# Depthwise sums of the last six jobs in PSUM banks, with two of their taps multiplied and added by GpSimd

## The chip, the core and the metric

The kernel runs on one core of one Trainium2 chip. The metric is the device time of one execution in microseconds. Engines are named as in the profile: PE (TensorE), DVE (VectorE), ACT (ScalarE), POOL (GpSimd), SP (SyncE); PEld is PE's weight load, and SPq is SP's queue of transfers.

## The reference

The input is 16 images of 128 channels and 96x96 pixels, in float32. Each image goes through one block: a normalisation over the channels, an attention over channels, a second normalisation, and a feed-forward part with a 3x3 depthwise convolution. Both halves add their result to their input.

```python
x_hwc = x.transpose(0, 2, 3, 1)
xn1 = _layernorm(x_hwc, ln1_w, ln1_b)
attn_out = _attention(xn1, wq, wk, wv, wp)       # 8 heads, softmax over a 16x16 matrix per head
x = x + attn_out.transpose(0, 3, 1, 2)
xn2 = _layernorm(x.transpose(0, 2, 3, 1), ln2_w, ln2_b).transpose(0, 3, 1, 2)
# _ffn: 128 -> 512 channels, 3x3 depthwise on 512, exact gelu, 512 -> 128 channels
h1 = jnp.einsum('bchw,oc->bohw', xn2, w_in[:, :, 0, 0])
h2 = lax.conv_general_dilated(h1, w_dw, (1, 1), ((1, 1), (1, 1)), feature_group_count=512, ...)
h3 = jax.nn.gelu(h2, approximate=False)
x = x + jnp.einsum('bchw,oc->bohw', h3, w_out[:, :, 0, 0])
```

## The kernel before

Channels lie on the 128 partitions. An image is cut into 8 bands of 12 rows (1152 pixels), a band into 3 units of 4 rows (384 pixels); the 16 images give 128 bands. The 512 hidden channels are 4 chunks of 128. A *job* is one chunk of one band, that is one depthwise convolution of 128x1152 values; there are 450 jobs, since in 62 of the 128 bands the fourth chunk is done by PE instead (L968, nine matmuls per unit with the first layer's weights folded into the taps). The last two bands are of that kind, so the last six jobs are chunks 0 to 2 of these two bands.

*Normalisations.* Both norms, called a (first) and b (second), run over groups of 512 pixels. PE transposes four blocks of 128 pixels into a PSUM tile `pT` (L610); DVE takes the statistics of two blocks at a time (`st`, L617); POOL adds the epsilon (L624) and raises to the power -1/2 (`rstd`, L628); for norm b DVE makes the shift (`nb`, L632). ACT writes the scaled blocks to SBUF (`zT`, L664 for a, L668 for b), and PE transposes three blocks back into a PSUM tile `pB` (`back`, L715), from which ACT places them in the padded input `xn` of the next stage (L721 for a, L719 and L725 for b). In norm a, PE also adds up the matrix of channel products (L678).

*PSUM.* There are eight banks of 512 float32 per partition. Two are the turning buffers of the pool `p_tr` (the tiles `pT`), one is the pool `p_bk` (`pB`), four are the tiles `h_0` to `h_3` that matmuls share, and one holds the products of norm a:

```python
p_tr = ctx.enter_context(tc.tile_pool(name="p_tr", bufs=2, space=PSUM))
p_bk = ctx.enter_context(tc.tile_pool(name="p_bk", bufs=1, space=PSUM))
...
d["pT", q] = p_tr.tile([P, QT, P], F32, tag="tr", name=f"pT_{name}_{q}")
...
d["pB"] = p_bk.tile([P, UT], F32, tag="bk", name=f"pB_{name}_{u}")
```

*A job.* PE multiplies the input with the chunk's weights (`hidden`, L900), ACT evicts the result to a padded tile (`kept`, L905). The nine taps of the convolution are shifted views of that tile; the first layer's weights are scaled so that tap 0 has the factor 1. DVE adds the taps one after the other with a multiply-and-add (`tap`, L918), the first of them onto tap 0. Taps 1 and 2 are multiplied by ACT (`product`, L913) into SBUF tiles `pr` and added by accumulating DMAs that POOL issues (`add_products`, L922: tap 2's product onto tap 1's, then the sum onto DVE's sum). DVE does six taps in each job, and eight in the very last, which has no DMA taps. Then ACT takes the gelu in place (L926), PE multiplies the four chunks with the output weights (`ffn_out`, L991), and the result is added to the residual, by ACT's copy (L1003) and a DMA (L1006), or in the last two bands by DVE (`add_here`, L998). SP stores the band.

*Order.* Nothing is left to a run-time scheduler. `Plan` collects every operation with its engine, a planned duration, a place in the order (the table `AT`), its reads and its writes, plays them through in planned time, and hands out buffer slots. The operations are then emitted in the order of their planned starts, and each engine works through its own list in that order. The waits between engines are put in by the framework when the program is built: it follows which instruction touches which tile, and adds a semaphore wait where two engines' uses of a tile must not overlap.

Of the kernel before, what the change touches and what calls it, by code (L numbers as in the profile page):

```python
# [18 lines left out]
BR = 12  # L19
PE_CHUNK = 3  # L20
PE_BANDS = (0, 2, 4, 6, 8, 10, 12)
PE_OF = 15
PE_LAST = (0, 1, 2, 4, 5, 7)
TINY = 1e-20
UNIT_MIN = 1e-18
DMA_TAPS = (1, 2, 3)
THIRD, THIRD_OF, THIRD_CHUNK = (), 3, 1
PART, Z_PARTS = 24, 6
QT, QB = 4, 1
# [11 lines left out]
    add_x_0=-281.3, gram_0=-43.8, forth_a_0=-74.3, forth_b_0=1.05, stats_a_0=-30.2, stats_b_0=-254.35,  # L41
    scaled_a_0=-88.5, scaled_b_0=171.2, back_a_0=-144.35, back_b_0=-18.9, place_a_0=-142.05, place_b_0=49.7,
    shift_b_0=-116.3, late=-68.9,
)
STEP = dict(scaled=0.3, hidden=0.1, products=0.5, tap=0.166, conv=1.6, conv_tap=0.03, out=0.8, out_part=0.05)
SLACK = 300
# [4 lines left out]
T_VARIANCE = 420  # L51
T_POWER = 1000
T_ADD, T_MOVE = 3100, 1800


class Plan:
# [154 lines left out]
def tile_restormer_block(  # L211
# [24 lines left out]
    nc = tc.nc  # L236
    B, C, H, W = x.shape
    P = 128
# [3 lines left out]
    UT = UR * W  # L242
# [11 lines left out]
    const = ctx.enter_context(tc.tile_pool(name="const", bufs=1))  # L254
    xpool = ctx.enter_context(tc.tile_pool(name="xpool", bufs=XB_BUFS))
    x1pool = ctx.enter_context(tc.tile_pool(name="x1pool", bufs=X1_BUFS))
    p_tr = ctx.enter_context(tc.tile_pool(name="p_tr", bufs=2, space=PSUM))
    p_bk = ctx.enter_context(tc.tile_pool(name="p_bk", bufs=1, space=PSUM))
    p_h = ctx.enter_context(tc.tile_pool(name="p_h", bufs=1, space=PSUM))
    p_g = ctx.enter_context(tc.tile_pool(name="p_g", bufs=1, space=PSUM))  # L260

    xbs, x1s = {}, {}
    banks = [p_h.tile([P, 4 * P], F32, name=f"h_{k}") for k in range(H_BANKS)]


# [20 lines left out]
    ratio = const.tile([P, NCH, 9], F32, name="ratio")  # L286
# [22 lines left out]
    prp = ctx.enter_context(tc.tile_pool(name="prp", bufs=PR_BUFS))  # L309
# [39 lines left out]
    op = plan.op  # L349

    def at(kind, place, i=1):
        return place + AT[kind if i else kind + "_0"]
# [25 lines left out]
    def dve(ns, p, f, r, w, two=False):  # L378
        op("DVE", ns, p, f, r, w, ns + 120 + SLACK, ns + 120, two=two)
# [7 lines left out]
    def act(ns, p, f, r, w):  # L387
        op("ACT", ns, p, f, r, w, ns + 150 + SLACK, ns + 150)
# [162 lines left out]
    def norm(i, second, place_of):  # L551
# [41 lines left out]
        def pixels(s, m):  # L593
# [8 lines left out]
            def forth(q):  # L602
                if early:
                    d["pT", q] = bank((name, q)).rearrange("p (t c) -> p t c", c=P)
                else:
                    d["pT", q] = p_tr.tile([P, QT, P], F32, tag="tr", name=f"pT_{name}_{q}")
                for k in range(QT):
                    b, j = divmod(q * QT + k, TPB)
                    xt = (xbs if x_key(i, b, second) == "xb" else x1s)[i, b]
                    nc.tensor.transpose(d["pT", q][:, k, :], xt[:, j * P : (j + 1) * P], ident)  # L610
# [96 lines left out]
        def channels(s, u):  # L707

            d = {}

            def back():
                d["pB"] = p_bk.tile([P, UT], F32, tag="bk", name=f"pB_{name}_{u}")
                for j in range(TPU):
                    q, k = divmod(u * TPU + j, QT)
                    nc.tensor.transpose(d["pB"][:, j * P : (j + 1) * P], zTs[q][:, k, :P], ident)  # L715

            def place():
                if second:
                    nc.scalar.activation(interior(i, u), rows(d["pB"]), AF.Identity, bias=b2)  # L719
                else:  # L720
                    nc.scalar.copy(interior(i, u), rows(d["pB"]))  # L721

            def place_row(k, r, row):
                to = window(xns[k], r, 1, 1)
                nc.scalar.activation(to, rows(d["pB"])[:, row : row + 1, :], AF.Identity, bias=b2)  # L725

            copies = []
            if second and u % UPP == 0 and u > 0:
                copies.append((part_of(i, u * UR - 1)[0], PART + 1, 0, UPP))
            if second and u % UPP == UPP - 1 and u < NU - 1:  # L730
                copies.append((part_of(i, (u + 1) * UR)[0], 0, UR - 1, -1))

            pb = ("bk", (name, u))
            quads = {(u * TPU + j) // QT: None for j in range(TPU)}
            pe(110 * TPU, at("back" + ab, s, i), back, [(*zt_of(q), k) for q in quads for k in range(2)], [pb])
            act(t_act(UT, 1) - 43 if second else t_copy(UT), at("place" + ab, s, i), place, [pb, ("w", "shift")], [z_unit(i, u)])
            for k, r, row, of in copies:
                act(225, at("place" + ab, s, i), lambda k=k, r=r, row=row: place_row(k, r, row), [pb, ("w", "shift")], [("z", k, of)])
# [138 lines left out]
    def h3_of(g, n):  # L877
        if (g, n) not in h3s:
            h3s[g, n] = h3p.tile([P, BR, W], F32, tag="h3", name=f"h3_{g}_{n}")
        return h3s[g, n]  # L880

    def conv_job(j, g, n):

        i, b = divmod(g, NB)
        kz, r0 = part_of(i, b * BR)
        xn = xns[kz]
        d = {}
        jn = (g, n)
# [14 lines left out]

        def kept(r, e):
            nc.scalar.copy(window(h1_, r, e - r, 1), rows(d.pop(("ph", r))))  # L905

        def shifted(t):
            dy, dx = divmod(t, 3)
            return window(h1_, dy, BR, dx)

        def product(t):
            to = d["pr", t] = prp.tile([P, BR, W], F32, tag="pr", name=f"pr_{g}_{n}_{t}")
            nc.scalar.activation(to, shifted(t), AF.Copy, scale=ratio[:, n, t : t + 1])  # L913

        def tap(t):
            h3 = h3_of(g, n)
            onto = shifted(0) if t == left[0] else h3
            nc.vector.scalar_tensor_tensor(h3, shifted(t), ratio[:, n, t : t + 1], onto, ALU.mult, ALU.add)  # L918

        def add_products(t):  # L920
            to = d["pr", DMA_TAPS[0]] if t != DMA_TAPS[0] else h3_of(g, n)
            nc.gpsimd.dma_start(out=to, in_=d["pr", t], accum_op=ALU.add)  # L922

        def gelu(s0, s1):
            h3 = h3_of(g, n)[:, s0 * UR : s1 * UR, :]
            nc.scalar.activation(h3, h3, AF.Gelu)  # L926

        last = j == len(jobs) - 1
        third = n == THIRD_CHUNK and g % THIRD_OF in THIRD
        dma_taps = () if last else DMA_TAPS[: 3 if third else 2]  # L930
        left = [t for t in range(1, 9) if t not in dma_taps]
        h1 = [("h1", n, k) for k in range(4)]
        h3 = [("h3", jn, s) for s in range(UPB)]
        for k, (r, e) in enumerate(chunks):
            ph = ("h", (jn, r))
            jk, zs = j + STEP["hidden"] * k, z_units(kz, r0 + r, r0 + e)
            to = h1[k + 1 : k + 2] if r else h1[:2]
            pe(t_mm((e - r) * W), at("hidden", jk), lambda r=r, e=e: hidden(r, e), [*zs, ("w", "in")], [ph])
            act(t_copy((e - r) * W), at("kept", jk), lambda r=r, e=e: kept(r, e), [ph], to)
        for k, t in enumerate(dma_taps):  # L940
            jk = j + STEP["products"] * k
            act(t_act(BR * W, 1), at("products", jk), lambda t=t: product(t), h1, [("pr", (jn, t))])
        pr = [("pr", (jn, t)) for t in dma_taps]
        for k, t in enumerate(dma_taps[1:]):
            add(at("add_last", j), lambda t=t: add_products(t), [pr[1 + k]], [pr[0]])
        for k, t in enumerate(left):
# [143 lines left out]
```

## Time and profile before

| what | value |
|---|---|
| runs | 4182.61 and 4180.88 us, median 4181.74 |
| the profiled execution, its span | 4197.8 us |
| mean granted clock of PE | 0.996 |
| busy: PE | 4120.2 us, 98% |
| busy: DVE | 4089.8 us, 97% |
| busy: ACT | 3697.8 us, 88% |
| busy: POOL | 2606.6 us, 62% |
| DMA | 831.16 MB, mean 198 GB/s |

The span is counted from the first to the last instruction of one profiled execution; it is 16 us longer than the median of the runs. Busy shares are of the span. A row of the groups reads: line, engine, operation, what is written and read with the shapes, count, then total busy time and the mean duration of one in ns, then the idle time of the engine just before these instructions and what ended it. A row of the timeline reads: start and length in us, engine, line, operation, tiles, count; equal instructions that follow each other are one row.

### The profile page before, as it was taken

The numbers are of one execution on the slowest core, as the hardware profiler recorded it, in microseconds if no ns is written. First come the engines' busy times: TensorE is split into PE (matmuls) and PEld (weight loads), VectorE is DVE, ScalarE is ACT, GpSimd is POOL, SyncE is SP. The second block draws the span as 40 slices with busy tenths as digits, with TensorE's granted clock in tenths as the row PEclk, the third lists the DMA queues.
The fourth block names the chain that finished last, engine by engine and source line by source line (L and its number), as shares of the span: only waits on it lengthen the run. The fifth ranks groups of instructions, "written<-read, shape, count | busy, mean of one in ns | idle before, by whom it ended". The sixth has DMA issues, their size and how long they took to land.

```text
span 4197.8 us, 52159 instructions
## 1 busy us (share of the span) xinstructions
PE 4120.2 (98%) x17265; PEld 2648.1 (63%) x17265; DVE 4089.8 (97%) x4450; ACT 3697.8 (88%) x7232; POOL 2606.6 (62%) x2397
## 2 busy tenths in 40 slices
PE   8999999999999999999999999999999999999999
PEld 6666666666666666656666666666666666665555
DVE  6999999999999999999999999999999999999998
ACT  5899988999899888889899989998899888999885
POOL 4757666565666757767576565666656666675442
PEclk9999999999999999999999999999999999999999
DMA  3899999999999999999999999999999999999997
GB/s 91 178 195 213 194 215 196 198 203 204 205 206 202 209 193 205 198 211 202 195 210 205 204 203 199 210 199 210 200 204 208 194 212 200 201 203 191 196 190 167
DMA packets 204797, 831.16 MB, mean 198 GB/s; under 512 B 23664, under 2 KB 25072, under 8 KB 204528
## 3 DMA queue, kind: packets, MB, share of 16 engines
q0 software_dynamic: 165024, 676.01, 83.3%
q1 hardware_dynamic: 37152, 151.01, 9.8%
q8 instruction: 137, 2.24, 0.2%
q10 hardware_dynamic: 2352, 0.81, 0.1%
q14 instruction: 132, 1.08, 0.1%
HBM read 148.26 MB, written 75.50 MB: 53 GB/s over the span
## 4 chain that ended last, share of the span: by engine, by line
PE 59%; DVE 27%; ACT 5%; POOL 4%; DMA 2%; issue 2%; ACTq 0%; POOLq 0%; DVEq 0%
DVE h L918 24%; PE h L968 16%; PE h L991 15%; PE h L900 12%; PE g L678 4%; PE h L567 4%; PE pB_a L715 2%; PE pT_b L610 2%; PE pB_b L715 2%; PE pT_a L610 2%; DVE st_a L617 1%; DMA h<-pr 1%; DVE st_b L617 1%; ACT pr L913 1%; POOL rstd_b L628 1%
## 5 line engine op out<-in xcount | busy, mean ns | idle before, releaser
L918 DVE SCALAR_TENSOR_TENSOR h<-h,ratio,h 128x1152 f32<-128x1152 f32 x2252 | 3105.2, 1403 | 4.1
L913 ACT ACTIVATE pr<-h,ratio 128x1152 f32<-128x1152 f32 x898 | 1159.8, 1296 | 44.0 <-DMA h<-pr 29.8
L968 PE MATMUL h<-xn,comp 128*128 128x384 f32 x3348 | 1195.2, 486 | 2.5 <-ACT h L905 2.5
L991 PE MATMUL h<-h,woutT 128*128 128x384 f32 x3072 | 1138.7, 488 | 5.8 <-ACT h L926 2.8
L900 PE MATMUL h<-xn,winT 128*128 128x384 f32 (+1 forms) x2700 | 1073.2, 502 | 6.1 <-ACT h L905 3.4
L968 PEld LDWEIGHTS h<-xn,comp 128*128 128x128 f32 x3348 | 609.1, 190 | 369.0 <-issue 8.1
L991 PEld LDWEIGHTS h<-h,woutT 128*128 128x128 f32 x3072 | 559.6, 190 | 351.8 <-issue 11.6
L905 ACT COPY h<-h 128x384 f32<-128x384 f32 (+1 forms) x1350 | 667.5, 527 | 116.5 <-PE h L900 89.0
L922 POOL DMA_DIRECT2D h<-pr x449 | 436.4, 972 | 468.2 <-DVE h L918 140.2
L922 POOL DMA_DIRECT2D pr<-pr x449 | 441.9, 984 | 406.2 <-ACT pr L913 368.9
L900 PEld LDWEIGHTS h<-xn,winT 128*128 128x128 f32 x2700 | 480.7, 190 | 292.8 <-issue 45.1
L918 DVE SCALAR_TENSOR_TENSOR h<-h,ratio 128x1152 f32<-128x1152 f32 x450 | 631.1, 1407 | 11.9 <-PE h L991 5.3
L926 ACT ACTIVATE h<-h 128x1152 f32<-128x1152 f32 x452 | 545.3, 1209 | 13.8 <-DMA h<-pr 10.5
L628 POOL TENSOR_TENSOR rstd_a<-ve_a,mhalf 128x4 f32<-128x4 f32 x288 | 539.7, 1875 | 12.7
L628 POOL TENSOR_TENSOR rstd_b<-ve_b,mhalf 128x4 f32<-128x4 f32 x288 | 535.3, 1859 | 12.2
L624 POOL TENSOR_SCALAR ve_a<-st_a 128x4 f32<-128x4 f32 x288 | 340.9, 1184 | 260.9 <-DVE st_a L617 254.0
L668 ACT ACTIVATE zT<-pT_b,nb_b,rstd_b 128x128 f32<-128x128 f32 x1132 | 432.8, 488 | 33.3 <-DVE nb_b L632 30.2
L624 POOL TENSOR_SCALAR ve_b<-st_b 128x4 f32<-128x4 f32 x288 | 325.8, 1131 | 194.5 <-DVE st_b L617 188.8
L664 ACT ACTIVATE zT<-pT_a,rstd_a 128x128 f32<-128x128 f32 x1080 | 317.3, 409 | 44.8 <-POOL rstd_a L628 43.0
L678 PEld LDWEIGHTS g<-zT 128*128 128x128 f32 x2304 | 296.5, 192 | 51.0 <-issue 4.3
L678 PE MATMUL g<-zT 128*128 128x129 f32 x2304 | 306.5, 276 | 0.0
L567 PE MATMUL h<-xn,mwT 128*128 128x384 f32 x768 | 294.1, 496 | 11.7 <-ACT h L905 6.6
(175 smaller groups left out, 3710.6 us busy)
## 6 DMA issues: line engine op xcount, KB each, us to landing
pr<-pr POOLq DMA_DIRECT2D x449, 576.0 KB, 7.0
h<-pr POOLq DMA_DIRECT2D x449, 576.0 KB, 7.1
x<-in_x_dram SPq DMA_DIRECT2D x128, 576.0 KB, 6.4
out_dram<-x SPq DMA_DIRECT2D x127, 576.0 KB, 7.0
x<-out POOLq DMA_DIRECT2D x126, 576.0 KB, 7.4
x<-in_x_dram POOLq DMA_DIRECT2D x122, 576.0 KB, 7.2
out_dram<-x SPq DMA_DIRECT2D x3, 192.0 KB, 1.9
weights<-in_L_conv_w_in_dram ACTq DMA_DIRECT2D x1, 256.0 KB, 2.7
```

The lines of the kernel that those rows point to most:

```text
L567: nc.tensor.matmul(rows(pm), lhsT=mats[i][0], rhs=interior(i, u), start=True, stop=True)
L624: nc.gpsimd.tensor_scalar(ve, d["mv"][:, :, 2], 1.0 / C, EPS, ALU.mult, ALU.add)
L628: nc.gpsimd.tensor_tensor(rstd, d["ve"], mhalf, ALU.pow)
L678: nc.tensor.matmul(grams[i][:, : P + 1], lhsT=zt[:, :P], rhs=zt, start=(q == 0 and k == 0), stop=(q == NU * TPU // QT - 1 and k == QT - 1),)
L900: nc.tensor.matmul(rows(ph), lhsT=winT[:, n, :], rhs=window(xn, r0 + r, e - r, 1), start=True, stop=True)
L905: nc.scalar.copy(window(h1_, r, e - r, 1), rows(d.pop(("ph", r))))
L913: nc.scalar.activation(to, shifted(t), AF.Copy, scale=ratio[:, n, t : t + 1])
L918: nc.vector.scalar_tensor_tensor(h3, shifted(t), ratio[:, n, t : t + 1], onto, ALU.mult, ALU.add)
L922: nc.gpsimd.dma_start(out=to, in_=d["pr", t], accum_op=ALU.add)
L926: nc.scalar.activation(h3, h3, AF.Gelu)
L968: nc.tensor.matmul(d["pc"], lhsT=comp[:, t, :], rhs=window(xn, r0 + dy, UR, dx), start=(t == 0), stop=(t == 8),)
L991: nc.tensor.matmul(rows(d["po"]), lhsT=woutT[:, n, :], rhs=h3s[g, n][:, s * UR : (s + 1) * UR, :], start=(k == 0), stop=(k == NCH - 1),)
```

## The change

In the last six jobs (`BY_POOL = 6`) the taps 2 and 3 leave DVE and the DMA path. POOL multiplies tap 2 (`pool_product`) and adds tap 0 to it; ACT multiplies tap 3, and POOL adds that product too (`pool_sum`). DVE adds the remaining taps one after the other (`tap_sum`): the first is added to POOL's sum and written to PSUM, the next ones go from PSUM to PSUM, and the last is written to the job's tile in SBUF. Tap 1 still goes through ACT and an accumulating DMA, except in the very last job, where DVE does it. In the plan, the sums hold both slots of `tr` and the slot of `bk` from the first of the six jobs to the last.

A sum of 1152 float32 takes three neighbouring banks. So the pools `p_tr` and `p_bk` are replaced by one tile of three banks, `low`, for the whole kernel: the transposes of all norms now write to regions of it, the slot being the one that the plan has handed out. Lines behind the new code move down in the changed kernel (L918 becomes L923, L991 becomes L1023, and so on).

```diff
+BY_POOL = 6
+POOL_TAPS = (2, 3)
...
+    pool_tap=0.0,
...
+T_POOL_PRODUCT, T_POOL_SUM = 1500, 2600
...
-    p_tr = ctx.enter_context(tc.tile_pool(name="p_tr", bufs=2, space=PSUM))
-    p_bk = ctx.enter_context(tc.tile_pool(name="p_bk", bufs=1, space=PSUM))
+    p_low = ctx.enter_context(tc.tile_pool(name="p_low", bufs=1, space=PSUM))
...
+    low = p_low.tile([P, 3 * 4 * P], F32, name="low")
...
-                    d["pT", q] = p_tr.tile([P, QT, P], F32, tag="tr", name=f"pT_{name}_{q}")
+                    k = plan.slot["tr", (name, q)]
+                    d["pT", q] = low[:, k * 4 * P : (k + 1) * 4 * P].rearrange("p (t c) -> p t c", c=P)
...
-                d["pB"] = p_bk.tile([P, UT], F32, tag="bk", name=f"pB_{name}_{u}")
+                d["pB"] = low[:, 8 * P : 8 * P + UT]
...
+        def tap_sum(k, t):
+            onto = d["pr", "pool"] if k == 0 else low[:, : BR * W].rearrange("p (r w) -> p r w", w=W)
+            to = h3_of(g, n) if k == len(left) - 1 else low[:, : BR * W].rearrange("p (r w) -> p r w", w=W)
+            nc.vector.scalar_tensor_tensor(to, shifted(t), ratio[:, n, t : t + 1], onto, ALU.mult, ALU.add)
+
+        def pool_product(t):
+            to = d["pr", t] = prp.tile([P, BR, W], F32, tag="pr", name=f"pr_{g}_{n}_{t}")
+            nc.gpsimd.tensor_scalar(to, shifted(t), ratio[:, n, t : t + 1], 1.0, ALU.mult, ALU.mult)
+
+        def pool_sum(k, t):
+            to = d["pr", POOL_TAPS[0]]
+            nc.gpsimd.tensor_tensor(to, to, shifted(0) if k == 0 else d["pr", t], ALU.add)
+            d["pr", "pool"] = to
...
-        dma_taps = () if last else DMA_TAPS[: 3 if third else 2]
-        left = [t for t in range(1, 9) if t not in dma_taps]
+        by_pool = j >= len(jobs) - BY_POOL
+        dma_taps = () if last else DMA_TAPS[: 3 if third else 1 if by_pool else 2]
+        left = [t for t in range(1, 9) if t not in dma_taps and not (by_pool and t in POOL_TAPS)]
...
-        for k, t in enumerate(left):
+        if by_pool:
+            first_ = ("pr", (jn, POOL_TAPS[0]))
+            pool_by_act = POOL_TAPS[1:]
+            op("POOL", T_POOL_PRODUCT, at("pool_tap", j), lambda: pool_product(POOL_TAPS[0]), h1, [first_], ...)
+            op("POOL", T_POOL_SUM, at("pool_tap", j), lambda: pool_sum(0, 0), h1, [first_], ...)
+            for k, t in enumerate(pool_by_act):
+                act(t_act(BR * W, 1), at("products", j), lambda t=t: product(t), h1, [("pr", (jn, t))])
+                op("POOL", T_POOL_SUM, at("pool_tap", j), lambda t=t: pool_sum(1, t), [("pr", (jn, t))], [first_], ...)
+            sums = [("tr", "sum", 0), ("tr", "sum2", 0), ("bk", "sum", 0)]
+            for k, t in enumerate(left):
+                reads, writes = h1 + ([first_] if k == 0 else sums), h3 if k == len(left) - 1 else sums
+                dve(t_dve(BR * W), at("tap", j + STEP["tap"] * k), lambda k=k, t=t: tap_sum(k, t), reads, writes, k == 0)
+        for k, t in enumerate(left if not by_pool else ()):
```

More of the change, by code (lines that the diff above doesn't have):

```diff
@@ L945, in conv_job @@
             add(at("add_last", j), lambda t=t: add_products(t), [pr[1 + k]], [pr[0]])
-        for k, t in enumerate(left):
+        if by_pool:
+            first_ = ("pr", (jn, POOL_TAPS[0]))
+            pool_by_act = POOL_TAPS[1:]
+            op("POOL", T_POOL_PRODUCT, at("pool_tap", j), lambda: pool_product(POOL_TAPS[0]), h1, [first_], T_POOL_PRODUCT + SLACK)
+            op("POOL", T_POOL_SUM, at("pool_tap", j), lambda: pool_sum(0, 0), h1, [first_], T_POOL_SUM + SLACK)
+            for k, t in enumerate(pool_by_act):
+                act(t_act(BR * W, 1), at("products", j), lambda t=t: product(t), h1, [("pr", (jn, t))])
+                op("POOL", T_POOL_SUM, at("pool_tap", j), lambda t=t: pool_sum(1, t), [("pr", (jn, t))], [first_], T_POOL_SUM + SLACK)
+            sums = [("tr", "sum", 0), ("tr", "sum2", 0), ("bk", "sum", 0)]
[3 more added lines that the diff above has]
+        for k, t in enumerate(left if not by_pool else ()):
             dve(t_dve(BR * W), at("tap", j + STEP["tap"] * k), lambda t=t: tap(t), h1, h3, True)
```

## The prediction

> **What bounds the kernel now.** I read the page's head first, then the windows of the start, the steady part and the end, then the chain of waits, then the groups of the instructions that use the three PSUM banks, and last the timeline of one stretch.
>
> ```profile
> span 4197.8 us, 52159 instructions
> PE 4120.2 (98%) x17265; PEld 2648.1 (63%) x17265; DVE 4089.8 (97%) x4450; ACT 3697.8 (88%) x7232; POOL 2606.6 (62%) x2397
> ```
>
> The profiled execution took 4197.8 us; the two runs have a median of 4181.74, so 16 us are taken off a sum made against the trace. Two engines are full at once.
>
> ```profile
> core 0: us, PE busy (x) PEld busy (x) DVE busy (x) ACT busy (x) POOL busy (x), PEclk, DMA share, GB/s
> 0.00:105.00 105.00, 89.67 (x573) 73.40 (x574) 70.42 (x198) 53.56 (x137) 44.94 (x121) 0.98 0.30 91
> 105.00:4080.00 3975.00, 3916.34 (x16322) 2507.32 (x16321) 3914.68 (x4164) 3573.01 (x6980) 2529.28 (x2244) 1.00 0.96 202
> 4080.00:4198.00 118.00, 114.19 (x373) 67.41 (x371) 104.69 (x90) 71.25 (x118) 32.42 (x33) 1.00 0.79 172
> 3500.00:3580.00 80.00, 80.00 (x346) 52.33 (x345) 79.83 (x86) 70.79 (x139) 49.09 (x44) 1.00 0.96 201
> ```
>
> From 105 to 4080 us PE idles 59 us and DVE 60 us; in the stretch from 3500 to 3580 neither has anything to spare, and ACT has 9 us. A stall put on PE or DVE there is paid in full.
>
> The chain of waits, in order of time, tells what sets the end:
>
> ```profile
> 4178.06 1.29 PE h L968 x4
> 4179.35 14.85 PE h L991 x46
> 4194.20 0.02 issue
> 4194.23 0.56 DVE x L998
> ```
>
> PE works up to the last addition without a break (46 passes of 0.32 us). Taking work off DVE in the last two bands uncovers PE, whose work the change does not touch.
>
> **The change, part by part.** *The last six jobs.* DVE does 31 taps in place of 38 (five jobs 6 to 5, the last 8 to 6), ACT 11 products in place of 10, POOL 18 new operations of 1152 elements, and five of POOL's accumulating DMAs (the pr<-pr ones) go.
>
> ```profile
> L918 DVE SCALAR_TENSOR_TENSOR h<-h,ratio,h 128x1152 f32<-128x1152 f32 x2252 | 3105.2, 1403 | 4.1
> L573 DVE SCALAR_TENSOR_TENSOR x<-h,d,x 128x384 f32<-128x384 f32 x18 | 11.0, 616 | 3.1 <-PE h L567 3.0
> L922 POOL DMA_DIRECT2D pr<-pr x449 | 441.9, 984 | 406.2 <-ACT pr L913 368.9 <-DVE h L918 9.7 <-ACT zT L664 8.3
> L628 POOL TENSOR_TENSOR rstd_b<-ve_b,mhalf 128x4 f32<-128x4 f32 x288 | 535.3, 1859 | 12.2
> ```
>
> The first of these jobs has its input complete, and the last one its last tap, here (ACT's and DVE's timelines):
>
> ```profile
> 4120.06 0.48 ACT L905 COPY h<-h 128x384 f32<-128x384 f32 x1
> ```
>
> ```profile
> 4186.98 2.86 DVE L918 SCALAR_TENSOR_TENSOR h<-h,ratio,h 128x1152 f32<-128x1152 f32 x2
> ```
>
> Seven taps at 1.40 us are 9.8 us of DVE. A tap that goes through PSUM has no row of its size; it lies between the 1.40 of the SBUF tap and three times the 0.616 of the 384-element form from PSUM, 1.85, which over 31 taps would eat the gain and 4 us more. I take 1.40, the row of the same size. The 9.8 us lie behind PE (the chain above), so I enter 0. ACT's extra product is hidden in the 47 us that ACT idles after 4080. POOL's new operations are not in the trace: below, DVE's 1.40 each, 25 us in all; above, three times that, 76, since POOL takes 1.86 for only four elements. Freed of five issues at 0.98, POOL has the 70 us from 4120 to 4190 for them, beside some ten issues that stay. Each job's first tap waits for POOL's sum, and the other four queue behind it on DVE, then the gelu on ACT and PE's last products. At 25 us all is covered; at 76, with 10 of issues, POOL ends at 4206 and the last six taps (8.4) follow, some 25 us late. The kernel's planning constants (1.5 and 2.6 us) give 40. I enter 0 and keep -2 to +25.
>
> The Trainium skill, "GPSIMD Engine Reference", section "Instruction dispatch", gives about 2.5 cycles per element as the floor of a two-input operation, which at its 1.2 GHz is an estimated 2.4 us per sum; no row here shows it, and the sum would stay at 0.
>
> *Three banks in one tile.* This part acts in all 16 images. The order of instructions on every engine is the same as before until the last six jobs, but the waits are not. pT (two banks) and pB (one) were separate tiles; now all three are regions of `low`. In the changed program's list of waits, statistics on DVE that waited for PE alone now wait for ACT too, ACT's copies out of pB wait for DVE's statistics of pT, and PE's transposes into one bank wait for ACT's or DVE's reads of another. Any two engines' uses of `low` follow each other in program order, reads too. The groups concerned:
>
> ```profile
> L668 ACT ACTIVATE zT<-pT_b,nb_b,rstd_b 128x128 f32<-128x128 f32 x1132 | 432.8, 488 | 33.3 <-DVE nb_b L632 30.2 <-PE h L567 1.7 <-PE g L678 0.4
> L664 ACT ACTIVATE zT<-pT_a,rstd_a 128x128 f32<-128x128 f32 x1080 | 317.3, 409 | 44.8 <-POOL rstd_a L628 43.0 <-issue 0.9
> L719 ACT ACTIVATE xn<-pB_b,b 128x384 f32<-128x384 f32 x384 | 239.2, 623 | 33.8 <-PE pB_b L715 32.6
> L617 DVE BATCH_NORM_STATS2 st_b<-pT_b 128x6 f32<-128x256 f32 x566 | 236.6, 420 | 6.3 <-PE pT_b L610 6.3
> L617 DVE BATCH_NORM_STATS2 st_a<-pT_a 128x6 f32<-128x256 f32 x540 | 225.7, 419 | 15.1 <-PE pT_a L610 14.6 <-POOL ve_a L624 0.2
> L721 ACT COPY xn<-pB_a 128x384 f32<-128x384 f32 x384 | 201.6, 525 | 42.3 <-PE pB_a L715 41.2 <-PE h L968 0.2
> L715 PE MATMUL pB_a<-ident,zT 128*128 128x128 f32 x1152 | 195.7, 277 | 19.6 <-ACT zT L664 9.6 <-DVE zT L651 4.2 <-ACT xn L721 3.2
> L715 PE MATMUL pB_b<-ident,zT 128*128 128x128 f32 x1152 | 192.4, 274 | 7.8 <-ACT zT L668 4.4 <-ACT xn L725 2.9 <-ACT xn L721 0.3
> L610 PE MATMUL pT_b<-ident,x 128*128 128x128 f32 x1132 | 170.9, 274 | 5.2 <-ACT zT L664 3.8 <-ACT zT L668 0.8
> L610 PE MATMUL pT_a<-ident,x 128*128 128x128 f32 x1080 | 164.7, 275 | 2.6 <-ACT zT L664 1.7 <-ACT zT L668 0.6 <-DMA x<-in_x_dram 0.3
> ```
>
> Together 2,377 us of work that must take turns. How often that bites, I read by setting each instruction's new waits against the old timeline: where does the awaited instruction end after this one started? In these groups, 234 starts on PE come 133 us too early in sum, 386 on DVE 236 us, 417 on ACT 202 us: 571 us of overlap that the new waits forbid, 560 of it between 105 and 4080. A sum of overlaps is no time yet, since one engine's delay lets another catch up. So I worked one stretch through by hand, each start being the later of its old place plus its engine's delay and the end of what it awaits (plus 0.04).
>
> ```profile
> 3500.03 1.51 ACT L668 ACTIVATE zT<-pT_b,nb_b,rstd_b 128x128 f32<-128x128 f32 x4
> 3500.10 0.49 PE L715 MATMUL pB_a<-ident,zT 128*128 128x128 f32 x3
> ...
> 3502.56 0.50 ACT L721 COPY xn<-pB_a 128x384 f32<-128x384 f32 x1
> ...
> 3503.06 0.42 DVE L617 BATCH_NORM_STATS2 st_b<-pT_b 128x6 f32<-128x256 f32 x1
> ...
> 3504.62 0.60 ACT L719 ACTIVATE xn<-pB_b,b 128x384 f32<-128x384 f32 x1
> 3504.72 0.42 DVE L617 BATCH_NORM_STATS2 st_b<-pT_b 128x6 f32<-128x256 f32 x1
> ...
> 3505.10 1.15 ACT L664 ACTIVATE zT<-pT_a,rstd_a 128x128 f32<-128x128 f32 x4
> ...
> 3505.96 0.49 PE L715 MATMUL pB_b<-ident,zT 128*128 128x128 f32 x3
> ...
> 3506.94 0.60 PE L610 MATMUL pT_a<-ident,x 128*128 128x128 f32 x4
> ...
> 3507.24 0.62 ACT L719 ACTIVATE xn<-pB_b,b 128x384 f32<-128x384 f32 x1
> ...
> 3507.71 0.42 DVE L617 BATCH_NORM_STATS2 st_a<-pT_a 128x6 f32<-128x256 f32 x1
> 3507.71 0.39 ACT L725 ACTIVATE xn<-pB_b,b 128x96 f32<-128x96 f32 x1
> ```
>
> ACT's scalings at 3500.03 must await PE's transposes, done at 3500.59: ACT +0.6. Its copy then ends at 3503.65, and the statistics of 3503.06 await it: DVE +0.64. ACT's placing of 3504.62 ends at 3505.82; the statistics of 3504.72 await it: DVE +1.15, done at 3506.29. The scalings of 3505.10 await those: ACT +1.23, done at 3507.48. PE's transposes of 3505.96 await those: PE +1.56, so the ones of 3506.94 end at 3509.10; the placing of 3507.24 awaits them: ACT +1.9. The row copy then ends at 3510.0, and the statistics of 3507.71 await it: DVE +2.33. Behind each such wait stand the taps (DVE), the matmuls of L968, L991 and L900 (PE) and the evictions (ACT) that follow in the queue. Carried on to 3580, the delays are PE 4.15, DVE 4.8, ACT 4.15. This stretch holds 8.0 us of forbidden overlap, so a delay of about 4.5 is 0.56 of it.
>
> **The sum.** 560 x 0.56 = 314; the first 105 us, where PE and DVE idle, add perhaps 4; the last six jobs 0. 4197.8 + 318 = 4516 in the trace, less 16: 4500 us.
>
> The Trainium skill, "PSUM — Partial Sum Buffer", section "PSUM bank collisions raise a hardware error", says that engines must not meet in one bank and quadrant, while different banks run clean. The trace agrees: ACT's scalings of 3500.03 ran on pT's bank while PE wrote pB's at 3500.10. By that rule the chip needs none of the added waits; it makes the fourth case below.
>
> **The rivals.**
> - *Absorbed.* The delays become offsets between the engines, after which the same uses no longer meet. Then only the fullest engine's own overlap counts, less its idle time: DVE 236 - 60 = 176, or 4358 us. For it: clashes can space themselves out. Against: they go both ways between every pair of engines, so no constant offset removes them, and the stretch without idle gave more.
> - *Added up.* Each stall hits another engine at another place and nothing is recovered: 4182 + 571 = 4753. For it: 59 and 60 us of idle in 3975. Against: in the stretch worked through only 0.56 was left.
> - *Not slower.* The waits that bind hold bank by bank, as the rule has it, and those added end before their turn. Place: the uses of `low`; point of decision: the awaited end lies before the waiting start, as it does for all uses from 1000 to 1025 us, where I found no overlap. Then only the last six jobs are left, 0 to -9.8 us: 4172 to 4182, say 4180. Against: the 571 us.
>
> **How the numbers follow.** The worked stretch 0.60 with a range of its own of 4400 to 4640 (0.39 to 0.82 of the 560), absorbed 0.17, added up 0.15, not slower 0.08. The range goes from 4340, just under the absorbed case, to 4700, most of the way to the added-up one. About 2% (84 us) is what a measurement of this kernel can tell from no change: slower by more than that 0.92 (the first three), within it 0.07, faster 0.01, since the gain in the last six jobs is 9.8 us at most.
>
> **What would show it.** Right: the span grows evenly over the 16 images; PE's and DVE's busy time stays near 4120 and 4080 us while their shares fall to about 91%; before st_a and st_b on DVE, `low` on PE and zT and xn on ACT there is idle time released by ACT, PE or DVE uses of `low`, over 300 us on PE or DVE in all; the clock stays near 1.00. Wrong: a span up to 4080 like before's (the waits cost nothing), or most of the difference after the first of the last six jobs (then POOL's sums or the taps through PSUM were mispriced).

## The result, and the profile after

The changed kernel takes 4443.87 us (two runs, 4442.2 and 4445.54) against 4181.74 before: ratio 1.0627, 95% interval 1.0596 to 1.0658, slower. The forecast was 4500 with a range of 4340 to 4700. Both sides of this ratio rest on two runs. In 48 later runs the kernel before took 4186 to 4209 us, so the two of 4181 and 4183 were its quickest; by the later medians of about 4197 the change costs 247 us, not 262. The profiled execution is the first of the changed kernel's two runs. The page's head and the busy times:

```profile
span 4440.4 us, 52312 instructions
PE 4182.8 (94%) x17265; PEld 2618.4 (59%) x17265; DVE 4121.4 (93%) x4443; ACT 3737.8 (84%) x7233; POOL 2641.5 (59%) x2410
```

The span grew by 242.6 us. PE, which idled 77.6 us of the span before, now idles 257.6; DVE went from 108.0 to 319.0. PE's busy time also grew, by 62.6 us, though its rows did not: the rows of the two transposes (L615 and L720) add up to 737.4 us against 723.7 in the four rows of before, and those of the large matmuls are unchanged within 3 us each. All rows of PE together add up to 6912 us, far more than the busy time, since the profile's times of neighbouring matmuls overlap; with pauses between them they would overlap less. That reading of the 62.6 us is an argument and was not tried.

Where did the time go in? The windows of four stretches, each cut at the same instructions in both kernels (PE's counts in brackets agree). First before, then after:

```profile
core 0: us, PE busy (x) PEld busy (x) DVE busy (x) ACT busy (x) POOL busy (x), PEclk, DMA share, GB/s
105.00:1068.00 963.00, 942.25 (x3951) 602.59 (x3950) 947.55 (x1018) 865.46 (x1701) 611.07 (x546) 0.99 0.94 199
1068.00:2092.00 1024.00, 1008.17 (x4246) 647.46 (x4245) 1009.05 (x1079) 920.85 (x1808) 673.36 (x586) 1.00 0.96 203
2092.00:3116.00 1024.00, 1013.70 (x4284) 653.36 (x4283) 1013.42 (x1086) 931.89 (x1833) 657.41 (x592) 1.00 0.97 204
3116.00:4080.00 964.00, 952.22 (x3848) 603.91 (x3847) 944.65 (x984) 854.80 (x1640) 587.43 (x522) 0.99 0.95 199
```

```profile
110.86:1137.30 1026.44, 959.15 (x3951) 597.36 (x3950) 957.51 (x1019) 875.66 (x1702) 612.16 (x546) 0.99 0.89 187
1137.30:2220.60 1083.30, 1024.38 (x4246) 641.09 (x4245) 1017.02 (x1078) 931.90 (x1808) 660.57 (x586) 1.00 0.91 192
2220.60:3308.80 1088.20, 1030.84 (x4283) 643.88 (x4282) 1022.49 (x1086) 942.36 (x1834) 663.85 (x592) 1.00 0.91 192
3308.80:4315.40 1006.60, 961.49 (x3848) 595.88 (x3847) 951.47 (x984) 861.94 (x1639) 584.83 (x522) 1.00 0.91 191
```

The stretches grew by 63.4, 59.3, 64.2 and 42.6 us: 229.5 in the 3975 us ahead of the last six jobs, spread over all images. Before them lie 5.9 us (105.0 against 110.86), behind them some 7. The granted clock (PEclk) is the same, so the clock is not the cause. At each of the cuts PE, DVE and ACT are late by the same amount within 1 us (at the last one 235.4, 235.2 and 235.4): they fall behind in lockstep.

What do the engines wait for? The groups of the instructions that use `low`, and the new ones of the last six jobs:

```profile
L673 ACT ACTIVATE zT<-low,nb_b,rstd_b 128x128 f32<-128x128 f32 x1132 | 430.3, 475 | 61.1 <-DVE st_a L622 25.2 <-DVE nb_b L637 20.2 <-PE low L720 4.6
L720 PE MATMUL low<-ident,zT 128*128 128x128 f32 x2304 | 397.7, 282 | 157.5 <-DVE st_a L622 41.3 <-ACT zT L669 39.2 <-DVE st_b L622 34.8
L615 PE MATMUL low<-ident,x 128*128 128x128 f32 x2212 | 339.7, 277 | 51.2 <-DVE st_b L622 15.4 <-ACT zT L673 9.1 <-DVE st_a L622 7.3
L622 DVE BATCH_NORM_STATS2 st_b<-low 128x6 f32<-128x256 f32 x566 | 240.8, 427 | 137.5 <-PE low L720 37.6 <-ACT zT L669 34.9 <-ACT xn L724 17.9
L622 DVE BATCH_NORM_STATS2 st_a<-low 128x6 f32<-128x256 f32 x540 | 230.0, 427 | 108.2 <-ACT zT L669 28.8 <-ACT zT L673 23.2 <-PE low L720 17.1
...
L928 DVE SCALAR_TENSOR_TENSOR low<-h,ratio,low 128x1152 f32<-128x1152 f32 x19 | 27.0, 1423 | 0.6
L936 POOL TENSOR_TENSOR pr<-pr,h 128x1152 f32<-128x1152 f32 x6 | 16.3, 2712 | 0.3
L932 POOL TENSOR_SCALAR pr<-h,ratio 128x1152 f32<-128x1152 f32 x6 | 16.1, 2680 | 2.6 <-ACT h L910 2.1 <-ACT pr L918 0.5
L928 DVE SCALAR_TENSOR_TENSOR low<-h,ratio,pr 128x1152 f32<-128x1152 f32 x6 | 11.6, 1934 | 15.0 <-POOL pr L936 14.9
```

Durations of the old operations hardly moved (statistics 427 ns against 420). Idle time did: ahead of DVE's statistics 245.7 us against 21.4 before, ahead of PE's transposes 208.7 against 35.2. The names behind the arrows tell why. Before, statistics waited for the transposes into their own bank (L610). Now their first releasers are PE's back-transposes (L720), ACT's scalings (L669, L673) and ACT's placing (L724): uses that the kernel before did not make them wait for, and those of ACT are reads. PE's back-transposes, in turn, wait for DVE's statistics.

The stretch that the prediction worked through (3500 to 3510 before) lies here in the changed kernel's timeline:

```profile
3710.42 0.49 PE L720 MATMUL low<-ident,zT 128*128 128x128 f32 x3
3710.95 1.51 ACT L673 ACTIVATE zT<-low,nb_b,rstd_b 128x128 f32<-128x128 f32 x4 [0.50 <-PE low L720]
...
3713.49 0.48 ACT L726 COPY xn<-low 128x384 f32<-128x384 f32 x1
3714.00 0.43 DVE L622 BATCH_NORM_STATS2 st_b<-low 128x6 f32<-128x256 f32 x1 [0.30 <-ACT xn L726]
...
3715.53 0.61 ACT L724 ACTIVATE xn<-low,b 128x384 f32<-128x384 f32 x1
3716.17 0.43 DVE L622 BATCH_NORM_STATS2 st_b<-low 128x6 f32<-128x256 f32 x1 [0.42 <-ACT xn L724]
3716.70 1.14 ACT L669 ACTIVATE zT<-low,rstd_a 128x128 f32<-128x128 f32 x4 [0.56 <-DVE st_b L622]
3717.89 0.55 PE L720 MATMUL low<-ident,zT 128*128 128x128 f32 x3 [1.31 <-ACT zT L669]
3718.93 0.60 PE L615 MATMUL low<-ident,x 128*128 128x128 f32 x4
3719.56 0.58 ACT L724 ACTIVATE xn<-low,b 128x384 f32<-128x384 f32 x1 [0.58 <-PE low L615]
...
3720.41 0.43 DVE L622 BATCH_NORM_STATS2 st_a<-low 128x6 f32<-128x256 f32 x1 [1.16 <-ACT xn L730]
```

The last figures in brackets are idle time and its releaser. Where ACT scaled one bank while PE wrote another, the two now take turns: 3710.42, then 3710.95. Each wait of the hand working is there, with the releaser that it named.

The end of the chain of waits has changed hands:

```profile
4432.32 1.43 DVE h L928
4433.77 0.53 ACT h L945
4434.31 0.04 issue
4434.35 2.22 PE h L1023 x6
4436.59 0.56 DVE x L1030
```

Before, 46 passes of PE without a break ended the program. Now DVE's last tap does, with a gelu and six passes behind it.

### The profile page after: what moved, and what is told of

Its sections match the earlier page's. It is cut to its first block, busy times and chain, and to the rows that moved or that the text cites. A ratio compares the mean times of both kernels' runs of the same rounds, so it can differ in the third digit from the quotient of the medians.

```text
span 4440.4 us, 52312 instructions
## 1 busy us (share of the span) xinstructions
PE 4182.8 (94%) x17265; PEld 2618.4 (59%) x17265; DVE 4121.4 (93%) x4443; ACT 3737.8 (84%) x7233; POOL 2641.5 (59%) x2410
## 5 line engine op out<-in xcount | busy, mean ns | idle before, releaser
L923 DVE SCALAR_TENSOR_TENSOR h<-h,ratio,h 128x1152 f32<-128x1152 f32 x2220 | 3070.3, 1409 | 3.6
L918 ACT ACTIVATE pr<-h,ratio 128x1152 f32<-128x1152 f32 x899 | 1145.2, 1278 | 34.0 <-DMA h<-pr 23.9
L1023 PE MATMUL h<-h,woutT 128*128 128x384 f32 x3072 | 1138.5, 488 | 8.2 <-ACT h L945 6.5
L1023 PEld LDWEIGHTS h<-h,woutT 128*128 128x128 f32 x3072 | 558.8, 190 | 353.3 <-ACT h L945 14.6
L910 ACT COPY h<-h 128x384 f32<-128x384 f32 (+1 forms) x1350 | 653.3, 514 | 120.9 <-PE h L905 88.6
L923 DVE SCALAR_TENSOR_TENSOR h<-h,ratio 128x1152 f32<-128x1152 f32 x444 | 624.5, 1411 | 5.6 <-ACT h L910 5.0
L945 ACT ACTIVATE h<-h 128x1152 f32<-128x1152 f32 x452 | 533.2, 1181 | 15.7 <-DMA h<-pr 12.4
L720 PE MATMUL low<-ident,zT 128*128 128x128 f32 x2304 | 397.7, 282 | 157.5 <-DVE st_a L622 41.3
L720 PEld LDWEIGHTS low<-ident,zT 128*128 128x128 f32 x2304 | 270.7, 141 | 448.9 <-DVE st_b L622 83.8
L629 POOL TENSOR_SCALAR ve_a<-st_a 128x4 f32<-128x4 f32 x288 | 315.9, 1097 | 360.8 <-DVE st_a L622 359.4
L673 ACT ACTIVATE zT<-low,nb_b,rstd_b 128x128 f32<-128x128 f32 x1132 | 430.3, 475 | 61.1 <-DVE st_a L622 25.2
L615 PE MATMUL low<-ident,x 128*128 128x128 f32 x2212 | 339.7, 277 | 51.2 <-DVE st_b L622 15.4
L622 DVE BATCH_NORM_STATS2 st_b<-low 128x6 f32<-128x256 f32 x566 | 240.8, 427 | 137.5 <-PE low L720 37.6
```

Source lines behind the costliest of these rows:

```text
L629: nc.gpsimd.tensor_scalar(ve, d["mv"][:, :, 2], 1.0 / C, EPS, ALU.mult, ALU.add)
L673: nc.scalar.activation(zT(q)[:, k, :P], d["pT", q][:, k, :], AF.Identity, bias=d["nb"][:, t : t + 1], scale=d["rstd"][:, t : t + 1],)
L1023: nc.tensor.matmul(rows(d["po"]), lhsT=woutT[:, n, :], rhs=h3s[g, n][:, s * UR : (s + 1) * UR, :], start=(k == 0), stop=(k == NCH - 1),)
```

## The experiments

All use the same input as before; "before" is the kernel before, run on the same chip beside them. Its median there was 4196.45, 4197.96 and 4196.54 us in the three groups of runs. A difference in us is worked out from the ratio and these medians. The times expected for the first four runs were reckoned from 4182 us, some 15 below the median that these runs were then set against. For three of them, one tile, three tiles and the late tile, the measured time lies above the stated range; the differences from before (expected 236, 0 and 7; measured 238, 3 and 8) were met. In the runs with one tile, three tiles and pairs of banks, every engine goes through its instructions in the order of before, as their traces show.

### Is it the one tile, or the last six jobs?

The theory: the program makes any two engines' uses of one tile take turns, in whatever bank they lie. The rival: the banks themselves, or the new work on POOL.

**One tile, old last jobs.** The three banks stay one tile, but no job uses POOL:

```diff
-BY_POOL = 6
+BY_POOL = 0
```

> The norms' three banks in the one tile, the last six jobs as before. Theory one tile (any two engines' uses of the tile take turns, whatever the bank): it has the 571 us of forbidden overlap of the changed kernel and no new tail, so nearly all of the loss: the trace of the changed kernel is 235.6 us behind at the last transposes, so 4182 + 236 = 4418 us (4405 to 4430). Rival last jobs (POOL's products and sums, or the sums through PSUM, cost the time): 4182.

Measured: 4434.26 us, ratio 1.0567 (1.0545 to 1.0590), +238 us. Nearly all of the loss is here, without any sum in PSUM.

**Three tiles, old last jobs.** The same banks, fixed slots and order, but a tile for each bank:

```diff
-    low = p_low.tile([P, 3 * 4 * P], F32, name="low")
+    lows = [p_low.tile([P, 4 * P], F32, name=f"low_{k}") for k in range(3)]
...
+                    d["pT", q] = lows[k].rearrange("p (t c) -> p t c", c=P)
...
+                d["pB"] = lows[2][:, :UT]
```

> As the kernel with one tile, but the three banks are three fixed tiles of a bank each, handed out by the plan's slots. Theory one tile: no wait is added that ends late by the old timeline (forbidden overlap 0), so the time of before, 4182 (4175 to 4190). Rival fixed tiles (it is giving up the turning pools for hand-placed tiles that costs, not the joining of banks): about 4418, like the kernel with one tile.

Measured: 4201.4 us, ratio 1.0007 (0.9992 to 1.0023), the same as before. One of the two statistics groups, with one tile and then with three:

```profile
L622 DVE BATCH_NORM_STATS2 st_b<-low 128x6 f32<-128x256 f32 x566 | 240.3, 426 | 139.2 <-PE low L720 37.8 <-ACT zT L669 34.6 <-ACT xn L724 17.9
```

```profile
L623 DVE BATCH_NORM_STATS2 st_b<-low 128x6 f32<-128x256 f32 x566 | 236.9, 421 | 6.3 <-PE low L616 5.9
```

(The row names every tile of that pool `low`, whatever its number.) 139.2 us of idle time fall to 6.3, and the only releaser left is the transpose into the same bank. The memory and the work are the same in both kernels; what differs is which region carries a name of its own. So the rival "banks" falls, and so does fixed slots in place of turning pools, which these three tiles have too. The loss is one of the program's waits.

**The last six jobs alone.** The whole change to the last six jobs, but the norms keep their pools, and the large tile is opened when the first sum needs it:

```diff
+    early_pools = ctx.enter_context(ExitStack())
+    p_tr = early_pools.enter_context(tc.tile_pool(name="p_tr", bufs=2, space=PSUM))
+    p_bk = early_pools.enter_context(tc.tile_pool(name="p_bk", bufs=1, space=PSUM))
...
+    def low_sum():
+        if "low" not in late:
+            early_pools.close()
+            p_low = ctx.enter_context(tc.tile_pool(name="p_low", bufs=1, space=PSUM))
+            late["low"] = p_low.tile([P, 3 * 4 * P], F32, name="low")
```

> The whole change to the last six jobs, but the norms keep their pools, and the three-bank tile is opened only when the norms are done. Theory one tile: the loss of 236 us goes, and what is left is the last six jobs alone: the trace of the changed kernel falls a further 6.8 us behind after the last transposes, so 4182 + 7 = 4189 (4180 to 4195). Rival last jobs: 4440, like the changed kernel. My own forecast of no cost at the end would give 4182.

Measured: 4207.35 us, ratio 1.0020 (1.0008 to 1.0033), +8.4 us (3 to 14 by the interval). That agrees with the 9.6 us between the changed kernel and the first experiment (4443.87 and 4434.26). The two parts, 238 and 8.4, add up to 246; the change is 247 above this median of before, 262 above its own.

### How does the loss depend on which banks are tied?

In these three kernels, too, the last six jobs are those of before.

**Two slots of `pT` in one tile, `pB` in its own.**

```diff
-    low = p_low.tile([P, 3 * 4 * P], F32, name="low")
+    low = p_low.tile([P, 2 * 4 * P], F32, name="low")
+    low_b = p_low.tile([P, 4 * P], F32, name="low_b")
...
+                d["pB"] = low_b[:, :UT]
```

> As the kernel with one tile, but pT's two banks in one tile and pB in a tile of its own. Theory one tile: the forbidden overlap falls from 571 to 231 us (PE 37, DVE 139, ACT 55); at the 0.41 that the changed kernel paid of it that is 95 us: 4277 (4230 to 4320). If the loss goes with the number of engines in the chain and not with the overlap, it would be nearly all or nearly nothing: over 4380, or under 4200.

Measured: 4287.09 us, ratio 1.0219 (1.0199 to 1.0238), +92 us, near the 95 of the overlap rule.

**The first slot of `pT` with `pB`, the second alone.**

```diff
-    low = p_low.tile([P, 3 * 4 * P], F32, name="low")
+    low = p_low.tile([P, 2 * 4 * P], F32, name="low")
+    low_a = p_low.tile([P, 4 * P], F32, name="low_a")
...
+                    d["pT", q] = (low_a if k else low[:, : 4 * P]).rearrange("p (t c) -> p t c", c=P)
...
+                d["pB"] = low[:, 4 * P : 4 * P + UT]
```

> Another pair of banks in one tile: the first pT bank with pB, the second pT bank in a tile of its own. The last six jobs as before. Forbidden overlap 215 us (PE 70, DVE 60, ACT 85). Theory that all of it counts at the 0.41 to 0.42 of the two cases measured: 4196 + 88 = 4284 (4270 to 4295). Rival, that only PE's and DVE's part counts (those two are full, ACT is not), at the 0.52 of the other pair: 130 x 0.52 = 68, so 4264.

Measured: 4248.76 us, ratio 1.0116 (1.0097 to 1.0135), +49 us. Both numbers expected were missed. One kernel holds a tied and a free bank side by side, in its groups:

```profile
L623 DVE BATCH_NORM_STATS2 st_b<-low_a 128x6 f32<-128x256 f32 x294 | 124.9, 425 | 3.9 <-PE low_a L616 3.5
...
L623 DVE BATCH_NORM_STATS2 st_b<-low 128x6 f32<-128x256 f32 x272 | 116.0, 427 | 38.4 <-PE low L721 15.3 <-ACT xn L727 9.9 <-ACT xn L725 7.4
```

Statistics of norm b wait 3.9 us in the free bank and 38.4 in the tied one. The mechanism stands; the rule for its size does not.

**The second slot with `pB`.** The same edit with the two slots of `pT` exchanged:

```diff
+                    d["pT", q] = (low[:, : 4 * P] if k else low_a).rearrange("p (t c) -> p t c", c=P)
```

> The third pair: the second pT bank with pB in one tile, the first pT bank alone. Forbidden overlap 200 us (PE 65, DVE 57, ACT 78), nearly the mirror of the pair that cost 50.8 us. Theory that the loss follows the overlap of the pair: 4197 + 47 = 4244 (4235 to 4255), and the three pairs then add up to 91 + 51 + 47 = 189 of the 238 of the one tile, so that some 49 come from all three being tied at once. Rival, that the pairs simply add up: 238 - 91 - 51 = 96, so 4293.

Measured: 4240.34 us, ratio 1.0106 (1.0082 to 1.0130), +44.5 us, as the first of the two expectations had it. The three pairs cost 92, 49 and 44.5, together 185; all three banks in one tile cost 238. So 53 us come only when all are tied, and losses of pairs don't make up the whole.

### What happens in the last six jobs?

The theory after the late tile's +8.4 us: DVE waits for POOL's sums, and the saved taps gain nothing as PE sets the end. Its trace, a group and then DVE's and POOL's timelines (the eight taps from 4121.88 on in three pieces, so that the last two show singly):

```profile
L936 DVE SCALAR_TENSOR_TENSOR low<-h,ratio,pr 128x1152 f32<-128x1152 f32 x6 | 11.6, 1930 | 14.6 <-POOL pr L944 14.5
```

```profile
4115.23 5.39 DVE L931 SCALAR_TENSOR_TENSOR h<-h,ratio,h 128x1152 f32<-128x1152 f32 x4
...
4121.88 8.05 DVE L931 SCALAR_TENSOR_TENSOR h<-h,ratio,h 128x1152 f32<-128x1152 f32 x6
4129.97 2.26 DVE L931 SCALAR_TENSOR_TENSOR h<-h,ratio,h 128x1152 f32<-128x1152 f32 x1
4132.26 3.46 DVE L931 SCALAR_TENSOR_TENSOR h<-h,ratio,h 128x1152 f32<-128x1152 f32 x1
4143.34 1.43 DVE L936 SCALAR_TENSOR_TENSOR low<-h,ratio,pr 128x1152 f32<-128x1152 f32 x1 [7.62 <-POOL pr L944]
...
4160.98 4.45 DVE L936 SCALAR_TENSOR_TENSOR low<-h,ratio,pr 128x1152 f32<-128x1152 f32 x1 [1.54 <-POOL pr L944]
```

```profile
4122.84 8.19 POOL L940 TENSOR_SCALAR pr<-h,ratio 128x1152 f32<-128x1152 f32 x1 [2.15 <-DMA h<-pr]
...
4143.89 1.96 POOL L940 TENSOR_SCALAR pr<-h,ratio 128x1152 f32<-128x1152 f32 x1
...
4157.11 1.24 POOL L940 TENSOR_SCALAR pr<-h,ratio 128x1152 f32<-128x1152 f32 x1
```

DVE waits 14.5 us for POOL, half of it ahead of the first of the six jobs. There POOL's product takes 8.19 us, against 1.24 at 4157.11, where DVE's taps have their sum in PSUM. The two timelines show why. While the product is open, six old taps run at their usual length, 1.33 us apart, with no idle time between them. The product ends at 4131.03, just 1.06 us after the start of the seventh, which is the first with a gap (0.04 us) before it. That tap takes 2.26 us instead of 1.41, and the next one, beside POOL's first sum, 3.46. So POOL's work and a tap with both large inputs in SBUF take turns here: POOL gets in at a gap, and then DVE waits.

From the same old tap on (4113.30 before, 4115.23 here), DVE's last tap ends 7.8 us later than before. Seven taps saved are 9.8 us. Against them stand 9.2 us more of waiting (14.5 for POOL, where DVE had 5.3 for PE before), 5.9 us by which three taps were stretched (those two and the one at 4160.98), and some 2.5 us of smaller delays.

**No work on POOL, and none of its waits.** POOL's product and sums and ACT's product of tap 3 are left out in the last six jobs, so this kernel's result lacks their taps 2 and 3:

```diff
-            onto = d["pr", "pool"] if k == 0 else low_sum()
+            onto = shifted(0) if k == 0 else low_sum()
...
-            op("POOL", T_POOL_PRODUCT, at("pool_tap", j), lambda: pool_product(POOL_TAPS[0]), h1, [first_], ...)
-            op("POOL", T_POOL_SUM, at("pool_tap", j), lambda: pool_sum(0, 0), h1, [first_], ...)
...
```

> The last six jobs with POOL's product and sums left out, and ACT's product of tap 3 too (taps 2 and 3 are missing from these jobs' result); norms' pools kept. DVE does 31 taps instead of 38 and waits for nobody new. Theory PE sets the end: 4196, nothing gained. If DVE's taps were on the path: 4196 - 9.8 = 4186. With either, the difference to the version with POOL's work (8.4 us over before) is what waiting for POOL costs.

Measured: 4198.5 us, ratio 0.9998 (0.9985 to 1.0010). The end of its chain of waits:

```profile
4179.66 14.85 PE h L1026 x46
4194.51 0.02 issue
4194.53 0.56 DVE x L1033
```

It is the chain of before, down to the 46 passes of 14.85 us. Seven taps of DVE are gone for good here, and nothing is gained. So POOL's work, with ACT's product for it, costs the 8.4 us, and the taps that it relieves were worth nothing. This run does not part the waiting from the stretched taps.

**Sums in SBUF.** As the late tile, but the sums go to the job's own tile instead of PSUM:

```diff
-            onto = d["pr", "pool"] if k == 0 else low_sum()
-            to = h3_of(g, n) if k == len(left) - 1 else low_sum()
+            onto = d["pr", "pool"] if k == 0 else h3_of(g, n)
+            to = h3_of(g, n)
```

> The new last six jobs with POOL's work, but DVE's sums run in the job's SBUF tile, and no tile of three banks exists. In the traces of the changed kernel POOL's first product takes 8.2 to 8.5 us and the later ones 1.2 to 2.0, and the first ran beside DVE taps that read both inputs from SBUF. Theory contention (POOL and such taps stand in each other's way): most of the 18 POOL operations and the taps beside them get several times longer, 4196 + 25 (4210 to 4240). Rival first use (the 8 us are paid once, by the first operation of its kind): as with the sums in PSUM, 4205 (4200 to 4210).

Measured: 4219.6 us, ratio 1.0058 (1.0037 to 1.0080), +24 us, 16 more than with the sums in PSUM. Its groups:

```profile
L936 DVE SCALAR_TENSOR_TENSOR h<-h,ratio,h 128x1152 f32<-128x1152 f32 x25 | 59.7, 2389 | 0.8
L944 POOL TENSOR_TENSOR pr<-pr,h 128x1152 f32<-128x1152 f32 x6 | 19.1, 3182 | 0.3
```

A tap takes 2.39 us in the mean with the sum in SBUF, and 1.42 with the sum in PSUM (L928 above). POOL's sums go from 2.71 (L936 above) to 3.18. The mean of 2.39 mixes two kinds. By the trace, the 14 of the 25 taps that run beside a product or sum of POOL take 2.26 to 3.77 us; the 11 others, among them all of the last job, for which POOL has nothing left to do, take 1.40 to 1.42. So the rival, that only a first use is dear, falls: taps of all five earlier jobs are long, just where POOL works beside them. The Trainium skill, "SBUF — State Buffer", section "Who interferes with whom", says that a DVE instruction with two SBUF inputs contends with a GpSimd instruction that reads SBUF, and that one with at most one such input does not, certain modes of DVE apart; these rows agree. Where the result goes is not what counts: the late tile's tap at 4160.98 read both inputs from SBUF, wrote to PSUM and was stretched to 4.45 us, while its taps from `low` back to SBUF took 1.40 to 1.42. (Why POOL got in ahead of that one tap, and not ahead of others like it, the trace does not show.)

**The last job alone.** As the late tile, with `BY_POOL = 1`:

> The new way for the very last job alone, with the norms' pools kept: DVE does 6 taps there instead of 8, on a tile in PSUM. If PE sets the end, as in the chain of before, the time of before, 4196 (4190 to 4200). If DVE's last taps set it, 2 taps less: 4193. If waiting for POOL's sum costs more than two taps save: 4200.

Measured: 4197.53 us, ratio 0.9995 (0.9983 to 1.0007). Fewer taps on DVE, and no gain. From its timelines of DVE and POOL (five old taps in a row, of which the first three and the fourth are shown):

```profile
4172.88 4.33 DVE L931 SCALAR_TENSOR_TENSOR h<-h,ratio,h 128x1152 f32<-128x1152 f32 x3
4177.24 2.26 DVE L931 SCALAR_TENSOR_TENSOR h<-h,ratio,h 128x1152 f32<-128x1152 f32 x1
...
4176.30 2.00 POOL L940 TENSOR_SCALAR pr<-h,ratio 128x1152 f32<-128x1152 f32 x1
```

POOL's first product of this kernel runs beside DVE's old taps too, and takes 2.00 us, not 8.19. Here these taps have gaps of 0.04 us between them and come 1.45 us apart, so the product waits for one tap only. It ends at 4178.30, again 1.06 us after a tap's start (4177.24), and that tap again takes 2.26 us. The changed kernel and the one with sums in SBUF show the same 1.06 us behind the first tap with a gap. So the long first product is no matter of a first use: it waits as long as DVE's taps leave no gap. That is read from four traces; no run was made for it alone.

### Would the taps be worth something if PE had less to do?

**A band less on PE, in the late tile and in the kernel before.** The same edit in both; the fourth chunk of the eighth band from the end then goes to DVE instead of PE:

```diff
-PE_LAST = (0, 1, 2, 4, 5, 7)
+PE_LAST = (0, 1, 2, 4, 5)
```

> The new last six jobs with the norms' pools kept and the three-bank tile opened late, and one band fewer given to PE (the eighth from the end), so that PE has 27 matmuls less (17 us) and DVE one job more (6 taps, 8.4 us). If the seven taps saved at the end can be spent once PE has less to do: 4207 - 8 = 4199, about the time of before. If the waits for POOL hold DVE, now with more to do: 4215.

> The kernel before with the same band taken from PE and given to DVE, nothing else changed. PE and DVE idle about the same before, 59 and 60 us in the steady part, so moving 17 us of PE to 8.4 us of DVE should leave DVE the longer one: 4197 + 4 (4193 to 4208). If PE alone sets the end: 4180.

Measured: 4219.31 us with the late tile, ratio 1.0061 (1.0041 to 1.0080), and 4216.69 in the kernel before, ratio 1.0050 (1.0034 to 1.0066). The first is near the rival's number. DVE's wait for POOL's sums is the same as ever:

```profile
L936 DVE SCALAR_TENSOR_TENSOR low<-h,ratio,pr 128x1152 f32<-128x1152 f32 x6 | 8.6, 1425 | 14.6 <-POOL pr L944 14.6
```

The second missed its expectation: taking a band from PE costs 21 us by itself. The edit does more than move one chunk. The plan places every band by the mean number of jobs per band, which one more job changes, and in the traces the order of the instructions differs from that of before from about 200 us on, on PE, DVE, ACT and POOL. By 2000 to 3000 us the same statistics already start 5 to 16 us late. The 21 us are then not a price of the last bands alone; what in the new order costs them is not settled. So these two do not show what the taps would be worth with PE relieved; they show only that this way of relieving it isn't one. No version here beats the kernel before.

## Why the prediction was right, and where not

*The mechanism and its place: right.* One tile over three banks makes engines take turns that have nothing to do with each other (238 us with one tile, a ratio of 1.0007 with three). It acts evenly over the images, at the uses that the prediction listed, and through its lockstep no engine gets ahead of the others.

*The hand working: right.* From 3500 to 3580 it gave PE 4.15, DVE 4.8 and ACT 4.15 us; the same instructions in the two traces are 4.0, 4.5 and 3.4 us later.

*The step that was off: 560 x 0.56.* It gave 314 us for the 3975 us ahead of the last six jobs; measured are 229.5, that is 0.41 of the overlap. The term was mis-sized, not misplaced. The stretch held 8.0 us of overlap in 80, while the whole has 560 in 3975, 0.14 per us: the stretch had less of it than the mean, and lost more of it. Scaled by its length instead, 4.5 in 80 would have come to 224. One stretch could not tell which of the two to use, and the experiments say that overlap is a poor scale: with pairs of banks tied, 231 us of overlap cost 92 (0.40), 215 cost 49 (0.23) and 200 cost 44.5 (0.22). DVE's own part of the overlap goes with the losses more closely (139, 60 and 57 us in the pairs, 236 for all three banks, against losses of 92, 49, 44.5 and 238), but that was seen afterwards and not tried. What sets the factor stays open.

*The smaller terms.* The first 105 us cost 5.9 where 4 was said. The last six jobs were entered at 0, kept between -2 and +25, and cost some 7 to 10: POOL's operations, bounded by 1.40 and 4.2 us, took 2.7 in the mean, and DVE waited 14.9 us for them. "At 25 us all is covered" looked at the sum of POOL's work, not at its first item, and no term stood for the two engines taking turns: the first product took 8.47 us, as it had to wait for a gap between DVE's taps, and the taps beside POOL's work got longer. A tap through PSUM, bounded by 1.40 and 1.85, takes 1.42; the choice of the row of the same size was right. That PE covers DVE's 9.8 us was right, as the run without POOL's work shows.

*The 16 us taken off.* They were wrong as a correction. The profiled execution of before took its 4197.8 us as one execution among others: in later runs the kernel before took from 4186 to 4209 us, and the changed kernel's profiled run of 4442.2 us has a span of 4440.4, so little lies around a span. Without them the forecast would have been 4516, a little further off: this error went the lucky way.

*What would show it.* Even growth and the unchanged clock: right. PE's busy time was to stay near 4120 and rose to 4182.8, so the shares are 94 and 93%, not 91. The idle time ahead of the uses of `low` is 245.7 us on DVE and 208.7 on PE, under the 300 named.

*The rivals.* Absorbed, 4358: the delays of the engines did not turn into lasting offsets; all three fell behind by the same amount, and 229.5 is more than the 176 that it counted, though near DVE's own 236 without its idle time taken off. Added up, 4753: 0.41 of the overlap was left, not all of it. Not slower, by bank: with three tiles the waits are gone and the time is that of before, so the chip needed none of them; but they were in the program.

## What to carry to other kernels

Banks that different engines use at the same time should be tiles of their own: the waits that this framework puts in go by tile, so a large tile over several of them turns harmless overlap into turns that full engines pay for. Where a large tile is needed in one stage only, close the small ones there and open it then; that took the cost here from 247 to 8 us. And before work is moved from a full engine to another, look whose work ends the chain: if it is another engine's, the relief is worth nothing, and what it costs remains.

## What the runs showed of the hardware that was not expected

DVE's multiply-and-add with both large inputs in SBUF and POOL's elementwise work on SBUF took turns, a whole instruction at a time. Taps of 1152 elements beside POOL's work took 2.26 to 3.77 us instead of 1.41. Which engine waits hung, in all cases but one tap, on a gap of 0.04 us: six taps without one kept POOL's product waiting for some 7 us and lost nothing themselves, while taps with one let POOL in each time and waited for it. With the running sum in PSUM the tap takes 1.42 beside the same work on POOL. So the PSUM sums of this change do have a worth of their own, 16 us of the whole kernel, but only next to work on POOL that was worth less than nothing here.
